# Normalized rows plus projection bias kept in DRAM, and a last stage in five parts

## The chip, the cores and the metric

The kernel runs on one core of a Trainium2 chip. The time is device time in microseconds (us) of one execution, as the median of several runs. The engines are named as in the profile: PE (TensorE, matmuls; PEld is its weight load), DVE (VectorE), ACT (ScalarE), POOL (GpSimd), and SP (SyncE, which here only issues transfers). Each engine takes its instructions in program order, and waits for another engine or for a transfer by semaphores.

## What is computed

Two transformer layers over four sequences of 512 rows of 512 numbers (2048 rows in all, float32). Each layer normalizes its input and adds an attention and a mixture of experts, both taken from the same normalized rows. Only layer 1 is touched:

```python
xn = _layernorm(x)
x = x + _L1_attn_ref(xn, ...) + _L1_ffn_ref(xn, ...)

def _L1_ffn_ref(x, router_w, router_b, expert_w, expert_b, proj_w, proj_b, norm_w):
    logits = einsum('bsd,de->bse', x, router_w) + router_b
    topk_vals, topk_idx = top_k(logits, 2)
    topk_w = softmax(topk_vals)
    ...
    expert_out = silu(einsum('td,edf->etf', xf, expert_w) + expert_b[:, None, :])
    combined = ...            # the two chosen experts' rows, weighted with topk_w
    out = einsum('bsd,df->bsf', combined, proj_w) + proj_b
    y = x + out               # x is the normalized row here
    rms = sqrt(mean(y * y) + 1e-6)
    return norm_w * (y / rms)
```

What the change moves is `x + proj_b`, the sum of the normalized row and the projection's bias.

## The kernel before

The rows lie in 16 tiles of 128 rows x 512 (`NT` = 16, number `n`). `acc` (in SBUF) holds the residual stream, `xnT` the transposed normalized rows of a layer.

**Layer 0** runs in 32 steps (8 groups of head pairs x 4 sequences). `schedule` hangs further jobs into places `(step, place)` of this loop: router, experts, and from step 29 on the start of layer 1. `next_layer(n)` (L938) makes tile n's normalized rows of layer 1: `layernorm` (L215) writes `xn` on DVE (L236), stores it to `xnd` in DRAM (L237), and `turn` transposes it on PE. Then POOL adds the attention's output bias to `acc` (L944) and SP stores that to `accd`. The expert stage of layer 1 gathers its inputs from `xnd`. Tiles 0 to 11 have this in steps 29 to 31; tiles 12 to 15 in the boundary between the layers (from L1428), where it alternates with `values(0, t)`, the first value products. In the same steps POOL computes the scalars of layer 0's query norms (L565, L566), which ACT (L675) and then DVE wait for. `begin_combine` (L908) loads the constants that these jobs use, and its pool `comb` holds one buffer of each kind.

**Layer 1** is a loop over 16 groups `g` of heads and 4 blocks `kc` of keys, 64 places `at[0]` to `at[63]`. A place has score products (L1224), two exponentials on ACT (`pT`, L1226), the context products (L1238) and, on DVE, sums of the exponentials (`pS`, L1244), with projections of the next group (`queries7`, L1200) and of the next sequence's values (`values7`, L1160 to L1174) in between. The values of the last sequence are made in places 46 and 47. Jobs hang into these places too: 36 expert tiles, which store their rows to `yd` in DRAM (L527), and then the mixing stage.

**Mixing stage**, for each tile n: `mix` gathers the two experts' rows of each token from `yd` with two indirect transfers on POOL (L534), loads the normalized rows from `xnd` (`xa`), weights the first row with its gate on DVE (L1340) and adds the second, weighted, on DVE (L1341), while POOL adds the projection bias to `xa` (L1342). `turn_mix` transposes the mixture on PE (L1349) and ACT evicts it (L1354). `project_mix` multiplies with the projection on PE (L1360), DVE adds the result to `xa` (L1361), ACT squares and sums, POOL makes the norm scalars (L1365, L1366). `finish_mix` scales on DVE (L1371) and adds to the output (L1296). The four parts of tile n hang at places `here` to `here + 3`, with `here = 48 + n * 13 // 16`. Row buffers and `xa` are double.

**Order.** The source fixes which job hangs where. The order of instructions on each engine is set by a scheduler, which may move an instruction before earlier ones of the source, unless it is pinned with `tc.keep_in_program_order`. In `mix` the first weightings of tiles 0 and 1 are pinned (L1339). PSUM banks are handed round: a matmul into a bank waits for the read of what lay in it before (`bank1("mm", ...)` for the products of values, queries, attention output and mixing alike).

A second path for very large scores stands further down in the file and is not touched.

Of the kernel before, what the change touches and what calls it, by code (L numbers as in the profile page):

```python
# [49 lines left out]
def two_layers(ctx: ExitStack, tc: tile.TileContext, a: dict, out: bass.AP, large: bass.AP):  # L50
# [80 lines left out]
    xnd = dram.tile([T, HID], F32, tag="xnd", name="xnd")  # L131
    yds = [dram.tile([NS * P, HID], F32, tag=f"yd{i}", name=f"yd{i}") for i in range(2)]

    accd = dram.tile([T, HID], F32, tag="accd", name="accd")

    def load_x(n):
# [75 lines left out]
        tc.keep_in_program_order(V.memset(turned, 1.0))  # L212
        V.tensor_scalar(turned[R:P, :], wcol[R:P, 0:1], wcol[R:P, 1:2], D * math.sqrt(D), ALU.mult, ALU.mult)

    def layernorm(n, pool, bank, scaled=False):  # L215

        pin = tc.keep_in_program_order if n < TC else (lambda x: x)
        st = small.tile([P, 6], F32, tag="st", name=f"st_{n}")  # L220
        pin(V.bn_stats(st, acc[:, n, :]))
        mv = small.tile([P, 2], F32, tag="mv", name=f"mv_{n}")
        V.bn_aggr(mv, st)
        V.tensor_scalar(mv[:, 1:2], mv[:, 1:2], 1e-5, None, ALU.add)
        G.tensor_tensor(mv[:, 1:2], mv[:, 1:2], nhalf[:, 0:1], ALU.pow)
        if scaled:
            G.tensor_scalar(mv[:, 0:1], mv[:, 0:1], mv[:, 1:2], -1.0, ALU.mult, ALU.mult)
        made = {}

        def rows():  # L230
            tag = "ctx" if n in (2, 3) else "xn"
            xn = made["xn"] = (wk0 if n in (2, 3) else pool).tile([P, HID], F32, tag=tag, name=f"xn_{n}")
            if scaled:
                A.activation(xn, acc[:, n, :], AF.Identity, scale=mv[:, 1:2], bias=mv[:, 0:1])
            else:
                pin(V.tensor_scalar(xn, acc[:, n, :], mv[:, 0:1], mv[:, 1:2], ALU.subtract, ALU.mult))  # L236
            (nc.scalar if TC <= n < 2 * TC else nc.sync).dma_start(out=xnd[ts(n, P), :], in_=xn)  # L237

        def turn():
            xn, tr = made["xn"], bank("tr", f"trx_{n}")  # L240
            for k in range(KC):
                pin(PE.transpose(tr[:, ts(k, P)], xn[:, ts(k, P)], ident))
            A.copy(xnT[:, :, ts(n, P)], tr.rearrange("p (k t) -> p k t", k=KC))
        return rows, turn


    def logits(b, w, m, pool, name, get, bank):
# [660 lines left out]
    def begin_combine():  # L908

        scratch.close()  # L910
        first = ctx.enter_context(tc.tile_pool(name="first1", bufs=1, side="right"))
        load_square(first, "wvT")
        rout["rw"] = load_few(first, "rw", E, a["rw"])
        rout["rb"] = load(first, "rb", [P, E], a["rb"].partition_broadcast(P))
        rout["wo_b"] = load(first, "wo_b", [P, HID], a["wo_b"].partition_broadcast(P))
        rout["pool"] = scratch.enter_context(tc.tile_pool(name="comb", bufs=1, side="right"))
        rout["ex"].pool = rout["pool"]
# [18 lines left out]
        jobs0.append((at[n + 1], lambda n=n: rout.pop(n)()))  # L936

    def next_layer(n, pool, bank):  # L938
        make_rows, turn_ = layernorm(n, pool, bank)

        def rows():
            make_rows()

            G.tensor_tensor(acc[:, n, :], acc[:, n, :], rout["wo_b"], ALU.add)  # L944
            nc.sync.dma_start(out=accd[ts(n, P), :], in_=acc[:, n, :])
        return rows, turn_

    norms = {}
# [376 lines left out]
    def begin_mixing():  # L1325
        scratch.close()
        rout["mix"] = scratch.enter_context(tc.tile_pool(name="mix", bufs=2, side="right"))
        rout["ex1"].pool = rout["mix"]
        load_square(rout["mix"], "pw")
        for nm in ("pb", "nw1"):  # L1330
            rows[nm] = load(rout["mix"], nm, [P, HID], a[nm].partition_broadcast(P))

    def mix(n):

        g0, g1 = rout["ex1"].gather(n)
        x = rout["mix"].tile([P, HID], F32, tag="xr", name=f"xa_{n}")
        nc.sync.dma_start(out=x, in_=xnd[ts(n, P), :])

        pin = tc.keep_in_program_order if n < 2 else (lambda x: x)  # L1339
        pin(V.tensor_scalar(g0, g0, r1.gate[:, 0, n : n + 1], None, ALU.mult))  # L1340
        V.scalar_tensor_tensor(g0, g1, r1.gate[:, 1, n : n + 1], g0, ALU.mult, ALU.add)  # L1341
        G.tensor_tensor(x, x, rows["pb"], ALU.add)  # L1342
        held[n] = g0, x

    def turn_mix(n):
        g0, x = held[n]
        tr = bank1("mm", f"trc_{n}")
        for f in range(KC):
            PE.transpose(tr[:, ts(f, P)], g0[:, ts(f, P)], ident)  # L1349
# [6 lines left out]
    def project_mix(n):  # L1356
# [2 lines left out]
        for f in range(KC):  # L1359
            PE.matmul(op, lhsT=cT_[:, f, :], rhs=wa["pw"][:, f, :], start=(f == 0), stop=(f == KC - 1))  # L1360
        V.tensor_tensor(y, y, op, ALU.add)  # L1361
        sq = rout["mix"].tile([P, HID], F32, tag="th", name=f"ysq_{n}")
        ss = small.tile([P, 1], F32, tag="yss", name=f"yss_{n}")
        A.activation(sq, y, AF.Square, accum_out=ss)
        G.tensor_scalar(ss, ss, 1.0 / HID, 1e-6, ALU.mult, ALU.add)  # L1365
# [29 lines left out]
    for i, here in enumerate(here_):  # L1395
# [4 lines left out]
                ex.fetch_weights(j + 3)  # L1400
            ex.fetch_bias(i + 2)
        jobs1.append((at[here], after))
    first += 6 + NS * 11 // 12
    jobs1.append((at[first], begin_mixing))
    for n in range(NT):
        here = first + n * 13 // 16
        for d, f in ((0, mix), (1, turn_mix), (2, project_mix), (3, finish_mix)):
            jobs1.append((at[here + d], lambda n=n, f=f: f(n)))

    left_ = sums_qk()  # L1410
    for place, f in (((1, 1), left_[0]), ((1, 2), left_[1]), ((1, 3), left_[2]), ((2, 0), sums_v), ((2, 1), left_[3])):
# [4 lines left out]
        jobs1.append((place, lambda t=t: values(1, t)))  # L1416
    run1 = schedule(jobs1)

    values(0, 0)
    norm = [next_layer(3 * TC + t, rp, bank1) for t in range(2)]  # L1420
    norm[0][0]()
    values(0, 1)
    turn_ = second_logits(B - 2, rp, bank1)
    norm[0][1]()
    norm[1][0]()
    norm.append(next_layer(3 * TC + 2, rp, bank1))
    values(0, 2)
    turn_()  # L1428
    norm[1][1]()
    norm[2][0]()  # L1430
    norm.append(next_layer(3 * TC + 3, rp, bank1))
# [752 lines left out]
```

## Time and profile before

| what | value |
|---|---|
| median of 3 runs | 2073.92 us (2073.34 to 2074.24) |
| the profiled execution | 2074.66 us, its span 2072.6 us, PE clock 0.995 |
| busy PE / weight load / DVE / ACT / POOL | 2017.7 / 1205.3 / 1452.0 / 867.9 / 754.3 us |
| layer 0 / boundary / layer 1 | to about 1451 / 1451 to 1480 / from 1480 us |
| last expert rows stored, first gather of mixing issued | 1881.73 us |
| HBM read and written | 222.05 MB and 42.73 MB, 128 GB/s over the span |

Most groups of instructions of the mixing stage, and what the change adds to elsewhere, have simple durations when they stand alone:

| line | engine | what | us of one |
|---|---|---|---|
| L1340 | DVE | weight the first row | 0.48 |
| L1341 | DVE | add the second, weighted | 0.75 |
| L1342, L944 | POOL | add a bias, 128x512 | 1.26, 1.27 |
| L1354 | ACT | evict the transposed mixture, 128x512 | 0.60 |
| L1226 | ACT | exponential, 128x1024 | 1.01 |
| L1244 | DVE | sum of exponentials, 128x1024 | 1.22 |
| L534 | POOL | issue a gather of 128 rows | 1.16 mean |
| `accd`, `xnd` | SP | store of 256 KB, issue to landing | 2.0 median |

How to read the profile: a line of a timeline gives the start in us from the span's beginning, the duration, the engine, the source line, the operation, output <- inputs by the program's names, shapes, and, in brackets, how long the engine stood idle just before and what it waited for. A line of a window gives its bounds, its length, then the busy time (and number of instructions) of PE, PEld, DVE, ACT and POOL, the granted PE clock, the share of the DMA engines' time that was busy, and GB/s. A duration that is longer than the same instruction's elsewhere says that something held it while it ran; idle time in brackets says that something held it before it started. Idle time of an engine other than PE matters only where PE later waits for it.

### The profile page before, as it was taken

How to read it: one execution, taken by the hardware profiler on the slowest of the kernel's cores; microseconds unless marked ns; L12 is line 12 of the kernel's file. 1: busy time of each engine (PE TensorE's matmuls, PEld its weight loads, DVE VectorE, ACT ScalarE, POOL GpSimd, SP SyncE). 2: the span in 40 equal slices, each digit the busy share in tenths (PEclk: the TensorE clock that was granted, in tenths of full speed). 3: DMA queues.
4: the chain of work that ended last, by engine and by line, in shares of the span. 5: the costliest groups of instructions: out<-in, count | busy, mean ns of one | idle time of the engine just before them, and what ended most of it. 6: DMA issues, size and time to landing. Idle time of an engine off the chain costs nothing.

```text
span 2072.6 us, 27984 instructions
## 1 busy us (share of the span) xinstructions
PE 2017.7 (97%) x9130; PEld 1205.3 (58%) x9130; DVE 1452.0 (70%) x3543; ACT 867.9 (42%) x2600; POOL 754.3 (36%) x761
## 2 busy tenths in 40 slices
PE   6999999999999999999999999999999999999997
PEld 4666666666666666666666666666334445445442
DVE  7888967666766666676667778787596555557775
ACT  4554444444444443444444455454243432333332
POOL 4422244443423333344333444353114332332550
PEclk9999999999999999999999999999999999999999
DMA  7102133333333343234443222121317765773551
GB/s 250 68 31 62 42 118 120 143 108 103 130 130 104 109 155 103 92 135 166 183 170 116 70 76 85 42 72 62 119 51 244 263 243 196 257 243 123 158 163 52
DMA packets 98906, 267.23 MB, mean 129 GB/s; under 512 B 14400, under 2 KB 27840, under 8 KB 87488
## 3 DMA queue, kind: packets, MB, share of 16 engines
q0 software_dynamic: 27072, 148.91, 21.4%
q1 hardware_dynamic: 70528, 114.34, 16.4%
q10 hardware_dynamic: 1152, 2.10, 0.3%
q8 instruction: 75, 1.23, 0.2%
q14 instruction: 79, 0.65, 0.1%
HBM read 222.05 MB, written 42.73 MB: 128 GB/s over the span
## 4 chain that ended last, share of the span: by engine, by line
PE 81%; DVE 8%; ACT 3%; POOL 2%; DMA 2%; issue 1%; SPq 0%; ACTq 0%; POOLq 0%; DVEq 0%
PE p L661 23%; PE hp_r L518 12%; PE op L828 10%; PE st L753 4%; PE st L1224 3%; PE qp L1200 3%; PE sp L744 3%; PE cx L1238 2%; PE ca L797 2%; PE o L1307 2%; PE trm_r L506 2%; PE vp L1160 1%; PE trq L681 1%; PE trk L687 1%; PE cc L800 1%
## 5 line engine op out<-in xcount | busy, mean ns | idle before, releaser
L828 PE MATMUL op<-Wo,cT 128*128 128x512 f32 x512 | 230.6, 598 | 5.3 <-DVE lv L725 2.9
L518 PE MATMUL hp_r<-we_r,xT_r 128*128 128x512 f32 (+1 forms) x592 | 224.8, 596 | 0.0
L470 POOL DMA_INDIRECT xr_r<-xnd,rows_r x72 | 89.4, 1242 | 331.6 <-PE trm_r L506 298.2
L761 POOL TENSOR_TENSOR lT<-lT,lmask 128x512 f32<-128x512 f32 (+1 forms) x128 | 157.6, 1244 | 140.8 <-ACT lT L757 140.6
L661 PE MATMUL p<-wT,x 128*128 128x384 f32 x512 | 179.6, 493 | 0.5 <-DVE wT L119 0.5
L661 PE MATMUL p<-wB,x 128*128 128x384 f32 x512 | 175.9, 488 | 4.0 <-DVE u L717 4.0
L661 PE MATMUL p<-wA,xnT 128*128 128x384 f32 x512 | 174.0, 492 | 0.2 <-DVE u L696 0.2
L828 PEld LDWEIGHTS op<-Wo,cT 128*128 128x128 f32 x512 | 92.0, 190 | 115.0 <-issue 77.2
L564 ACT ACTIVATE sq<-qb 128x128 f32<-128x128 f32 x384 | 118.9, 310 | 93.0 <-DVE qb L710 44.9
L1226 ACT ACTIVATE pT<-st 128x1024 f32<-128x1024 f32 x128 | 123.7, 1014 | 62.7 <-PE st L1224 57.0
L518 PEld LDWEIGHTS hp_r<-we_r,xT_r 128*128 128x128 f32 (+1 forms) x592 | 83.8, 170 | 97.3 <-issue 91.8
L831 DVE TENSOR_TENSOR acc<-acc,op 128x512 f32<-128x512 f32 x128 | 87.4, 685 | 69.4 <-PE op L828 69.0
L661 PEld LDWEIGHTS p<-wB,x 128*128 128x128 f32 x512 | 93.9, 190 | 68.5 <-issue 10.2
L661 PEld LDWEIGHTS p<-wT,x 128*128 128x128 f32 x512 | 94.5, 193 | 63.5 <-issue 6.7
L661 PEld LDWEIGHTS p<-wA,xnT 128*128 128x128 f32 x512 | 95.6, 193 | 61.0 <-issue 2.9
L675 ACT ACTIVATE qb<-qb,ss 128x128 f32<-128x128 f32 x256 | 81.9, 390 | 110.7 <-POOL ss L566 108.6
L508 ACT COPY xT_r<-trm_r 128x512 f32<-128x512 f32 x72 | 41.8, 581 | 198.0 <-PE hp_r L518 188.3
L757 ACT ACTIVATE lT<-st,ss 128x256 f32<-128x256 f32 (+1 forms) x128 | 47.2, 449 | 175.4 <-PE st L753 175.3
L753 PE MATMUL st<-qkT 128*128 128x256 f32 (+1 forms) x512 | 110.4, 357 | 0.0
L534 POOL DMA_INDIRECT row_r<-yd,slot_r x64 | 74.2, 1160 | 94.0 <-DVE row_r L1341 35.8
L753 PEld LDWEIGHTS st<-qkT 128*128 128x128 f32 x512 | 93.1, 193 | 11.4 <-issue 1.4
L566 POOL TENSOR_TENSOR ss<-ss,nhalf 128x6 f32<-128x6 f32 x64 | 95.7, 1496 | 5.3
(360 smaller groups left out, 4334.2 us busy)
## 6 DMA issues: line engine op xcount, KB each, us to landing
x<-xsd SPq DMA_DIRECT2D x112, 256.0 KB, 3.1
yd<-yr_r SPq DMA_DIRECT2D x72, 256.0 KB, 3.4
wA<-in_wA SPq DMA_DIRECT2D x16, 384.0 KB, 3.6
wB<-in_wB SPq DMA_DIRECT2D x16, 384.0 KB, 7.6
xnd<-xn SPq DMA_DIRECT2D x24, 256.0 KB, 2.0
accd<-acc SPq DMA_DIRECT2D x18, 256.0 KB, 2.0
acc<-in_x SPq DMA_DIRECT2D x16, 256.0 KB, 4.9
Wo<-in_Wo SPq DMA_DIRECT2D x8, 512.0 KB, 3.6
```

What stands on the lines that cost most here:

```text
L470: G.indirect_dma_start(out=out, out_offset=None, in_=src, in_offset=at_rows(idx))
L518: PE.matmul(hp[ts(h, m), :], lhsT=xT[:, k, ts(h, m)], rhs=w[:, ts(k, HID)], start=(k == 0), stop=(k == KC - 1))
L534: G.indirect_dma_start(out=x, out_offset=None, in_=self.yd, in_offset=at_rows(self.r.slot[:, k, n : n + 1]))
L564: A.activation(sq, x[:, h, :], AF.Square, accum_out=ss[:, h : h + 1])
L566: G.tensor_tensor(ss, ss, nhalf[:, 0:n], ALU.pow)
L661: PE.matmul(p, lhsT=x[:, k, ts(c, P)], rhs=w[:, k, :], start=(k == 0), stop=(k == 1))
L675: A.activation(x[:, j, :], x[:, j, :], AF.Copy, scale=sq[t][:, j : j + 1])
L753: PE.matmul(st[:, ds((t % 2) * 256, n)], lhsT=qkT[:, HG + h, ts(t, P)], rhs=qkT[:, h, ds(t * P, n)], start=True, stop=True)
L761: G.tensor_tensor(dst, dst, lmask.rearrange("p a w j -> p (a w j)")[:, 0:n], ALU.mult)
L828: PE.matmul(op, lhsT=cT[:, h, ts(t, P)], rhs=wo[:, h, :], start=(h == 0), stop=(h == HG - 1))
L831: V.tensor_tensor(acc[:, n, :], acc[:, n, :], op, ALU.add)
L1226: A.activation(pt[:, ts(pair, 2), :], st, AF.Exp, scale=SCALE1)
```

## The change

Where layer 1's normalized rows are made (`next_layer`), POOL now also forms `xp = xn + pb`, tile by tile in one buffer, and SP stores it to a new DRAM tensor `xpd`. For this `pb` is loaded with the constants of `begin_combine`. In the mixing stage `xa` is loaded from `xpd`, and the POOL addition of the bias is gone.

The stage has five parts instead of four: `gather_mix` (the two gathers), `mix` (weighting: the first row now on ACT, a copy with a scale, the second on DVE as before), `turn_mix` (now also loads `xa`, in four buffers), `project_mix`, `finish_mix`. The stage begins one place earlier, at `at[47]`. For tiles 0 to 2 the gathers hang at 47, 47 and 48 and the weighting at 49; from tile 3 on the weighting, transposes, projection and finish are at the places where they were. The first row has three buffers instead of two, the square's scratch one instead of two, and the pin of the first weightings is gone. The norm's weights go into the buffer of the attention's output bias, which is free by then.

In the boundary between the layers, the normalizations of tiles 12 and 13 are set up before `values(0, 0)`, and the router's logits of sequence 2 are made before `values(0, 1)` and finished right behind it.

```diff
@@ setup
+    xpd = dram.tile([T, HID], F32, tag="xpd", name="xpd")
@@ layernorm
-    def layernorm(n, pool, bank, scaled=False):
+    def layernorm(n, pool, bank, scaled=False, made=False):
...
-        made = {}
+        of, made = made, {}
...
-        return rows, turn
+        return (rows, turn, made) if of else (rows, turn)
@@ begin_combine
         rout["rb"] = load(first, "rb", [P, E], a["rb"].partition_broadcast(P))
+        rout["pb"] = load(first, "pb", [P, HID], a["pb"].partition_broadcast(P))
         rout["wo_b"] = load(first, "wo_b", [P, HID], a["wo_b"].partition_broadcast(P))
@@ next_layer
-        make_rows, turn_ = layernorm(n, pool, bank)
+        make_rows, turn_, rows_ = layernorm(n, pool, bank, made=True)
...
             G.tensor_tensor(acc[:, n, :], acc[:, n, :], rout["wo_b"], ALU.add)
             nc.sync.dma_start(out=accd[ts(n, P), :], in_=acc[:, n, :])
+
+            xp = pool.tile([P, HID], F32, tag="xp", name=f"xp_{n}")
+            G.tensor_tensor(xp, rows_["xn"], rout["pb"], ALU.add)
+            nc.sync.dma_start(out=xpd[ts(n, P), :], in_=xp)
@@ -1325,25 +1332,29 @@
     def begin_mixing():
         scratch.close()
         rout["mix"] = scratch.enter_context(tc.tile_pool(name="mix", bufs=2, side="right"))
-        rout["ex1"].pool = rout["mix"]
         load_square(rout["mix"], "pw")
-        for nm in ("pb", "nw1"):
-            rows[nm] = load(rout["mix"], nm, [P, HID], a[nm].partition_broadcast(P))
+
+        rows["nw1"] = rout["wo_b"]
+        nc.sync.dma_start(out=rows["nw1"], in_=a["nw1"].partition_broadcast(P))
+
+    def gather_mix(n):
+
+        held[n] = []
+        for k in range(2):
+            x = rout["mix"].tile([P, HID], F32, tag=f"row{k}", name=f"row{k}_r1_{n}", bufs=3 - k)
+            G.indirect_dma_start(out=x, out_offset=None, in_=yds[1], in_offset=at_rows(r1.slot[:, k, n : n + 1]))
+            held[n].append(x)
 
     def mix(n):
 
-        g0, g1 = rout["ex1"].gather(n)
-        x = rout["mix"].tile([P, HID], F32, tag="xr", name=f"xa_{n}")
-        nc.sync.dma_start(out=x, in_=xnd[ts(n, P), :])
-
-        pin = tc.keep_in_program_order if n < 2 else (lambda x: x)
-        pin(V.tensor_scalar(g0, g0, r1.gate[:, 0, n : n + 1], None, ALU.mult))
+        g0, g1 = held[n]
+        A.activation(g0, g0, AF.Copy, scale=r1.gate[:, 0, n : n + 1])
         V.scalar_tensor_tensor(g0, g1, r1.gate[:, 1, n : n + 1], g0, ALU.mult, ALU.add)
-        G.tensor_tensor(x, x, rows["pb"], ALU.add)
-        held[n] = g0, x
 
     def turn_mix(n):
-        g0, x = held[n]
+        g0, _ = held[n]
+        x = rout["mix"].tile([P, HID], F32, tag="xr", name=f"xa_{n}", bufs=4)
+        nc.sync.dma_start(out=x, in_=xpd[ts(n, P), :])
         tr = bank1("mm", f"trc_{n}")
         for f in range(KC):
             PE.transpose(tr[:, ts(f, P)], g0[:, ts(f, P)], ident)
@@ -1359,7 +1370,7 @@
         for f in range(KC):
             PE.matmul(op, lhsT=cT_[:, f, :], rhs=wa["pw"][:, f, :], start=(f == 0), stop=(f == KC - 1))
         V.tensor_tensor(y, y, op, ALU.add)
-        sq = rout["mix"].tile([P, HID], F32, tag="th", name=f"ysq_{n}")
+        sq = rout["mix"].tile([P, HID], F32, tag="th", name=f"ysq_{n}", bufs=1)
         ss = small.tile([P, 1], F32, tag="yss", name=f"yss_{n}")
         A.activation(sq, y, AF.Square, accum_out=ss)
         G.tensor_scalar(ss, ss, 1.0 / HID, 1e-6, ALU.mult, ALU.add)
@@ -1400,12 +1411,14 @@
                 ex.fetch_weights(j + 3)
             ex.fetch_bias(i + 2)
         jobs1.append((at[here], after))
-    first += 6 + NS * 11 // 12
+    first += 5 + NS * 11 // 12
     jobs1.append((at[first], begin_mixing))
     for n in range(NT):
         here = first + n * 13 // 16
-        for d, f in ((0, mix), (1, turn_mix), (2, project_mix), (3, finish_mix)):
-            jobs1.append((at[here + d], lambda n=n, f=f: f(n)))
+        for d, f in ((0, gather_mix), (1, mix), (2, turn_mix), (3, project_mix), (4, finish_mix)):
+
+            place = max(here + d, first + 1 + d + (n > 2)) if d else here
+            jobs1.append((at[place], lambda n=n, f=f: f(n)))
 
     left_ = sums_qk()
     for place, f in (((1, 1), left_[0]), ((1, 2), left_[1]), ((1, 3), left_[2]), ((2, 0), sums_v), ((2, 1), left_[3])):
@@ -1416,16 +1429,16 @@
         jobs1.append((place, lambda t=t: values(1, t)))
     run1 = schedule(jobs1)
 
+    norm = [next_layer(3 * TC + t, rp, bank1) for t in range(2)]
     values(0, 0)
-    norm = [next_layer(3 * TC + t, rp, bank1) for t in range(2)]
     norm[0][0]()
+    turn_ = second_logits(B - 2, rp, bank1)
     values(0, 1)
-    turn_ = second_logits(B - 2, rp, bank1)
+    turn_()
     norm[0][1]()
     norm[1][0]()
     norm.append(next_layer(3 * TC + 2, rp, bank1))
     values(0, 2)
-    turn_()
     norm[1][1]()
     norm[2][0]()
     norm.append(next_layer(3 * TC + 3, rp, bank1))
```

## The prediction

> **What bounds the kernel now.** I read the page's busy totals and the chain that ended last, then windows by stage, then each engine's timeline where TensorE (PE) idles. Totals and chain:
>
> ```profile
> PE 2017.7 (97%) x9130; PEld 1205.3 (58%) x9130; DVE 1452.0 (70%) x3543; ACT 867.9 (42%) x2600; POOL 754.3 (36%) x761
> ...
> PE 81%; DVE 8%; ACT 3%; POOL 2%; DMA 2%; issue 1%; SPq 0%; ACTq 0%; POOLq 0%; DVEq 0%
> ```
>
> PE is the bound: 2017.7 of 2072.6 us. The edit leaves its matmuls alone, so it acts only through PE's idle time and granted clock. Windows (us, then busy time of PE, weight loads, DVE, ACT, POOL, then PE clock, DMA share, GB/s), for the end of layer 0, the start of mixing, and mixing:
>
> ```profile
> 1400.00:1450.00 50.00, 46.49 (x248) 31.04 (x248) 38.70 (x115) 22.67 (x71) 18.94 (x18) 1.00 0.17 64
> 1878.00:1905.00 27.00, 27.00 (x144) 16.62 (x136) 16.22 (x25) 8.15 (x10) 6.99 (x7) 1.00 0.42 147
> 1960.00:2020.00 60.00, 54.60 (x220) 25.15 (x213) 41.65 (x59) 22.10 (x40) 34.52 (x37) 0.97 0.53 158
> 2020.00:2051.00 31.00, 27.43 (x113) 9.33 (x112) 22.75 (x31) 10.86 (x20) 4.99 (x8) 1.00 0.14 49
> ```
>
> PE has no hole while mixing starts (27.00 of 27.00) and loses 9.0 us between 1960 and 2051. That 9.0 is what can be won; the hole-free 27 us are what can be spoilt. PE's waits from 1905 to 2051, totalled (us, times, longest), then two pieces of its timeline (start, us, line, in brackets the idle time and what ended it):
>
> ```profile
> PE po L1360 <- DVE acc L1296: 2.1, 1, 2.1
> PE qp L1200 <- DVE xnT L1296: 2.0, 1, 2.0
> PE st L1224 <- ACT pT L1226: 1.7, 1, 1.7
> PE po L1360 <- DVE xa L1361: 1.6, 3, 0.6
> ```
>
> ```profile
> 1889.40 1.89 PE L1160 MATMUL vp<-acc 128*128 128x256 f32 x8
> 1891.13 1.89 PE L1160 MATMUL vp<-acc,xnT 128*128 128x256 f32 x8
> 1892.85 3.60 PE L1307 MATMUL o<-woT,cT 128*128 128x512 f32 x8
> ```
>
> ```profile
> 1973.13 3.12 PE L1200 MATMUL qp<-xnT,wqT 128*128 128x256 f32 x8 [2.01 <-DVE xnT L1296]
> 1976.06 1.62 PE L1200 MATMUL qp<-acc 128*128 128x256 f32 x4
> ```
>
> The last pair took 3.12 and 1.62 us; the same matmuls at 1898.45 and 1900.28, behind no stall, took 1.99 and 1.03. So PE ran slow after the stall: 1.7 us more. Three waits (2016.60, 1973.13, 2035.70) hold most of the idle time.
>
> **Removed: work in the mixing stage.** Sixteen DVE weightings (L1340, 0.48 us, 7.7 us in all) go to ACT, and sixteen POOL additions (L1342) go. The additions cost more than their own time where they meet DVE. DVE, then POOL:
>
> ```profile
> 1968.40 2.29 DVE L1244 TENSOR_TENSOR pS<-pS,pT 128x1024 f32<-128x1024 f32 x1
> ```
>
> ```profile
> 1968.18 1.42 POOL L1342 TENSOR_TENSOR xa<-xa,pb 128x512 f32<-128x512 f32 x1 [1.61 <-DVE acc L1296]
> ```
>
> The pS addition beside L1342 took 2.29 us, alone (1971.27) 1.21: 1.08 lost. Stall by stall: before 1973.13 the DVE chain held one L1340 (0.48) and that 1.08, so 1.56 of 2.01 goes, and with so short a stall the 1.7 of slow clock: 3.25. Before 2016.60 L1341 took 1.76 instead of 0.75 beside L1342, and one L1340 stood in the queue: 1.5. The 1.67 at 2035.70 (0.9 of slow matmuls behind it) goes back to POOL's norm scalars, queued behind an L1342 for which POOL had idled 6.04 until its rows landed at 2025.74; DVE and ACT stand between, so I take half, 1.3. Three stalls on the residual addition L1361 (0.25, 0.47, 0.60) lose about 1.0. Sum 7.05; less 0.5 for ACT's added op, **-6.5 us**. Ends: all eight stalls of the stage with their slow clock, 8.9 + 4.7 = -13.6; only the two collisions, 1.08 + 1.01 = -2.1. The added ACT op has no row; its nearest are the 128x512 evictions combT (0.60) and ysq (0.63): 0.6. In steady state it stands between two exponentials (1.01 each) and waits for a gather whose buffer a transpose frees: 0.3 to issue + 3.7 to land + 0.6 + 1.0 = 5.6 us, against 9.56 from one transpose to the next (1918.92 to 1928.48). PE's own work covers it by 4 us, and I exclude a loss there.
>
> **Added: rows plus bias in layer 0 and at the boundary.** Per tile one POOL addition (nearest row L944, same size: 1.27 us) and one 256 KB store on SP (like accd: 2.0 us to land), with one buffer. Twelve fall in layer 0's last steps, where POOL is 38% busy and hides most. Tile 5's does not hide: the new program order puts it ahead of L565/L566, on which a chain to PE hangs. POOL, then DVE, then PE:
>
> ```profile
> 1406.98 1.51 POOL L944 TENSOR_TENSOR acc<-acc,wo_b 128x512 f32<-128x512 f32 x1 [7.69 <-DVE xn L236]
> ```
>
> ```profile
> 1407.28 1.43 DVE L574 TENSOR_TENSOR r<-qb,t 128x192 f32<-128x192 f32 x1
> 1408.63 0.35 DVE L575 TENSOR_TENSOR r<-qb,t 128x192 f32<-128x192 f32 x1
> ```
>
> ```profile
> 1413.94 1.56 PE L661 MATMUL p<-wB,x 128*128 128x384 f32 x4 [0.48 <-DVE u L717]
> ```
>
> L565 (1408.58, right behind L944) moves by 1.27; behind it ACT's scaling, DVE's L813 and L717 move too, and PE, already idle 0.48 there, gets +1.27. DVE is 77% busy (38.70 of 50), and L574 beside L944 took 1.43, its equal L575 0.35: again 1.08. I put one more such collision on PE's path: **+2.35**. Ends: 0 (no collision, and the chain's slack larger than the trace lets see) and 1.27 + 3 x 1.08 = +4.5, a collision at each of the three larger PE stalls of that stretch.
>
> [...]
>
> At the boundary tile 11's new store (waiting for POOL's addition, about 1455.2) goes into SP's queue ahead of three weight loads. wkT was issued at 1454.35 and wv_b at 1455.82, both now some 1.4 us later; v's addition (DVE L1148), which waited for wv_b until 1466.07, moves with it, and tile 12's rows wait for the pool that the store holds (1458.44 to about 1460.5). PE's stalls there (0.80, 0.68, 0.83, 0.68, 0.80) are on those engines, and tile 13's DVE rows now also wait for the single buffer. The new order of the four normalizations gives part back: **+1.6**, ends 0 and +4, both transfers' delay one after the other.
>
> **Moved: the first weightings.** Before, those of tiles 0 and 1 were pinned and ran at 1903.01, long after their rows had landed. The pin is gone. The changed program has DVE's first three combinations (successors of L1341) between the additions of values: L1165, combine 0, L1166, combine 1, L1167, combine 2, L1168, two pS, L1170. ACT's three weightings stand ahead of the next pair of exponentials. The rows cannot come earlier, since POOL waits for the last expert store:
>
> ```profile
> 1881.73 1.15 POOL L534 DMA_INDIRECT row_r<-yd,slot_r  x1 [21.74 <-DMA yd<-yr_r]
> 1883.18 0.95 POOL L534 DMA_INDIRECT row_r<-yd,slot_r  x1 [0.30 <-issue]
> ```
>
> The transfers issued from 1880 to 1892 show what that costs (last number: median us from issue to landing; two loads of xa beside them took 9.1):
>
> ```profile
> row_r<-yd,slot_r POOLq DMA_INDIRECT x4, 7.4
> ```
>
> Combine 0 needs the second gather: 1883.18 + 7.4 = 1890.6, + 0.75 = 1891.3; L1166 (0.69) then ends at 1892.0, and the vp product that reuses its bank starts at 1892.1 instead of 1889.40. Combine 1 has the fourth: 1885.69 + 7.4 = 1893.1, with L1167 to 1894.5. Combine 2's second row reuses combine 0's buffer: issued 1891.4, landing after 3.7 (the later median) at 1895.1; combine 2 to 1895.8, L1168 to 1896.4, two pS (2.36) to 1898.7, L1170 to 1899.3. PE's L1307 waits for L1170's bank: 1899.35 instead of 1892.85, 6.5 late. A stall of 2 us cost 1.7 of slow clock at 1973 and 0.07 at 2016.60; I take 1.0: **+7.5**. Ends: 3.3 to land, the shortest later gather, puts L1170 at 1895.7, +2.9 with no slow clock; 9.1 for the first and 4.8 (slowest later) for the last make 9.3 + 1.7 = +11.0.
>
> [...] The row at 1973.13 shows slowing after 2.0 us already. [...]
>
> **Sum.** +2.35 + 1.6 + 7.5 - 6.5 = +4.95 on the profiled span: 2072.6 + 4.95 = 2077.55; around the span lie 2.06 us (2074.66 in all), so 2079.6. The profiled run is 0.74 above the median of 2073.92, so **2078.9**.
>
> **Rivals.** What can be told from no change is 0.2%, 4.15 us: 2069.8 to 2078.1.
> A, faster: the first gathers land as fast as the later ones (3.3 to 3.7), since the bias no longer loads beside them. The start then costs 2.9, and DVE, ahead of its queue, leaves no stall in the stage: 2073.9 + 2.35 + 1.6 + 2.9 - 13.6 = 2067.2. It decides below about 4.4 us to landing. For it: DVE and POOL end the stage's stalls. Against: the new order queues four row loads beside the first gathers, the same 2 MB. 0.22.
> B, within 0.2%: the same early landing with my gain of 6.5: 2074.4. 0.20.
> C, larger loss: the ACT weighting, behind slow gathers, also holds the exponentials later on, so the stage gives 2.1 only and the five parts do not run ahead as their number says (a row buffer still comes free at a transpose): 2073.9 + 2.35 + 1.6 + 7.5 - 2.1 = 2083.3. For it: landing at 7.4 makes the 5.6 us chain 9.3 of 9.56. Against: later gathers land in 3.7. 0.13.
> The forecast has 0.45.
>
> **Numbers.** All low ends give 2065.8, all high ends 2091.3; 8 in 10 lie between 2067 and 2087. Slower: the forecast, most of it, and C, less small parts on the line: 0.54; within 0.2%: 0.22; faster: 0.24. The forecast's own range is 2075 to 2084.
>
> **What would show it.** Right: PE idle before vp at about 1890 and before L1307, named after the combinations or their gathers; DVE idle there on a DMA; no 2.01 at qp. Wrong: no idle of PE from 1878 to 1905 (then A or B), or idle at exponentials behind the ACT weighting in every group (C). In layer 0, no extra 1.3 at L661's stall would drop the first term.

## The result, and the profile after

The changed kernel takes 2079.06 us (median of 14 runs, 2076.41 to 2083.78) against 2074.07 (14 runs, 2070.62 to 2079.67). The ratio is 1.0021, 95% interval 1.0014 to 1.0028: slower by 2.9 to 5.8 us. Its profiled execution has a span of 2075.7 us, 3.1 more than before. (Two places in the description above: the eviction of the transposed mixture is on L1353, and the boundary begins with L1419.) Lines of the changed kernel stand 2 to 13 higher than the same lines before: L1340 is now ACT's L1351, L1341 is L1352, L1166 is L1173, L1170 is L1177, L1307 is L1314, L1360 is L1371.

Busy totals of the changed kernel, then four windows. They begin 2 to 5 us later than the windows of the kernel before. The work itself comes 1 to 14 us later at their bounds (worked out as in the table further down), so they tell where the holes are and not what each of them costs:

```profile
PE 2018.1 (97%) x9130; PEld 1205.8 (58%) x9130; DVE 1441.8 (69%) x3527; ACT 878.1 (42%) x2616; POOL 748.5 (36%) x761
```

```profile
1405.00:1452.00 47.00, 40.81 (x224) 28.06 (x223) 34.16 (x101) 21.07 (x65) 26.22 (x24) 0.96 0.27 99
1880.00:1907.00 27.00, 22.36 (x104) 13.80 (x101) 17.72 (x24) 6.44 (x8) 7.76 (x8) 0.94 0.47 166
1963.00:2023.00 60.00, 58.83 (x245) 26.64 (x248) 43.51 (x61) 28.18 (x49) 25.66 (x30) 1.00 0.50 153
2023.00:2054.00 31.00, 30.41 (x136) 10.65 (x129) 23.52 (x32) 13.81 (x25) 2.96 (x8) 1.00 0.19 62
```

The holes have moved. Between 1963 and 2054 PE now idles 1.8 us instead of 9.0, while mixing's start, which had none, has 4.6 us of idle time at a clock of 0.94. Layer 0's end has become worse too: PE idles 6.2 us of 47 at a clock of 0.96. In the kernel before it was 3.5 us of 45 at 1.00:

```profile
1405.00:1450.00 45.00, 41.49 (x229) 27.94 (x228) 35.68 (x106) 21.00 (x65) 18.94 (x18) 1.00 0.19 71
```

More exact than windows is a ledger. PE runs the same matmuls in all kernels here, so each one's start can be set against its start in the kernel before; how much later it comes, at the two ends of a stretch, tells what the stretch lost (+) or gave back (-). Worked out so from the traces, in us, with the stretches named by the times of the kernel before:

| kernel | layer 0, 1340-1425 | 1425-1444 | boundary, to 1482 | layer 1, to 1885 | mixing's start, to 1898 | to 1930 | mixing, to 2055 |
|---|---|---|---|---|---|---|---|
| before, a second trace | +0.26 | +0.01 | +0.01 | -0.43 | 0.00 | 0.00 | +1.16 |
| changed | +3.54 | +1.57 | +1.10 | -0.18 | +6.85 | +0.96 | -10.76 |
| pin3 | +3.53 | +3.21 | +1.38 | +0.16 | 0.00 | +5.89 | -11.11 |
| natural | +3.55 | +1.40 | +1.33 | +0.81 | 0.00 | 0.00 | -10.59 |
| xp_only | +3.54 | +3.22 | +0.54 | -0.14 | 0.00 | 0.00 | -6.68 |
| five_only | +0.23 | +2.79 | -1.19 | +0.85 | +13.20 | +0.83 | -5.65 |
| natural_xnd | +0.25 | -0.01 | -1.19 | -0.42 | 0.00 | 0.00 | -5.47 |
| pin3_xp_late | +0.23 | +3.13 | -1.20 | +30.92 | 0.00 | +4.79 | -10.57 |
| natural_late | +0.24 | -0.02 | -1.20 | -0.30 | 0.00 | 0.00 | -9.30 |
| late_dve | +0.23 | +3.16 | -1.20 | +0.48 | 0.00 | 0.00 | -9.28 |
| store_only | -0.08 | +1.37 | +4.59 | +1.02 | +6.84 | +0.93 | -10.56 |
| xa_pinned | +3.29 | +1.60 | +1.05 | -0.05 | +4.85 | +1.03 | -9.93 |
| old_boundary | +3.53 | +3.23 | +0.29 | -0.40 | +6.96 | +0.94 | -10.63 |

Where the work is the same the figures of the first and third to sixth columns repeat to some 0.5 us (layer 1's, to 1); mixing's differ by 1.2 between the two traces of the kernel before; the second column is spoken of at the end. How late PE is at 1340 already (-1.8 to +1.5 in these traces) is not in the table, so a row need not add up to the difference in span. Mixing's start in the changed kernel, POOL, DVE and PE:

```profile
1888.42 0.94 POOL L1345 DMA_INDIRECT row_r<-yd,slot_r  x1 [22.47 <-PE vp L1167]
1889.67 0.95 POOL L1345 DMA_INDIRECT row_r<-yd,slot_r  x1 [0.30 <-issue]
```

```profile
1896.96 0.75 DVE L1352 SCALAR_TENSOR_TENSOR row_r<-row_r,gate_r,row_r 128x512 f32<-128x512 f32 x1 [7.54 <-DMA row_r<-yd,slot_r]
1897.62 0.68 DVE L1173 TENSOR_TENSOR xnT<-vp,xnT 128x512 f32<-128x512 f32 x1
...
1901.30 0.75 DVE L1352 SCALAR_TENSOR_TENSOR row_r<-row_r,gate_r,row_r 128x512 f32<-128x512 f32 x1 [1.46 <-DMA row_r<-yd,slot_r]
...
1904.84 0.68 DVE L1177 TENSOR_TENSOR v<-xnT,vp 128x512 f32<-128x512 f32 x1
```

```profile
1893.54 1.99 PE L1167 MATMUL vp<-wvT,acc 128*128 128x256 f32 x8
1898.37 3.30 PE L1167 MATMUL vp<-acc 128*128 128x256 f32 x8 [2.83 <-DVE xnT L1173]
1901.46 2.31 PE L1167 MATMUL vp<-acc,xnT 128*128 128x256 f32 x8
1905.58 3.70 PE L1314 MATMUL o<-woT,cT 128*128 128x512 f32 x8 [1.80 <-DVE v L1177]
```

DVE stands 7.54 us in front of the first combination, which starts at 1896.96, when the rows of the second gather, issued at 1889.67, have landed. Behind it stands L1173, which reads the bank that PE's next value product needs: PE idles 2.83, then 1.80, and its products take 3.30 and 2.31 us instead of 1.89.

### The profile page after: what moved, and what is told of

The parts are those of the page before. It is cut to its first block, busy times and chain, and to the rows that moved or that the text cites. A ratio compares the mean times of both kernels' runs of the same rounds, so it can differ in the third digit from the quotient of the medians.

```text
span 2075.7 us, 27993 instructions
## 1 busy us (share of the span) xinstructions
PE 2018.1 (97%) x9130; PEld 1205.8 (58%) x9130; DVE 1441.8 (69%) x3527; ACT 878.1 (42%) x2616; POOL 748.5 (36%) x761
## 4 chain that ended last, share of the span: by engine, by line
PE 81%; DVE 7%; ACT 3%; POOL 2%; issue 2%; DMA 2%; ACTq 0%; DVEq 0%; POOLq 0%; SPq 0%
PE p L663 23%; PE hp_r L520 12%; PE op L830 10%; PE st L755 4%; PE st L1231 3%; PE qp L1207 3%; PE sp L746 3%; PE cx L1245 2%; PE ca L799 2%; PE trm_r L508 2%; PE o L1314 2%; PE po L1371 1%; PE trq L683 1%; DMA row_r<-yd,slot_r 1%; PE trk L689 1%
## 5 line engine op out<-in xcount | busy, mean ns | idle before, releaser
L830 PE MATMUL op<-Wo,cT 128*128 128x512 f32 x512 | 231.4, 600 | 5.3 <-DVE lv L727 3.2
L830 PEld LDWEIGHTS op<-Wo,cT 128*128 128x128 f32 x512 | 92.2, 190 | 115.1 <-issue 77.2
L567 POOL TENSOR_SCALAR ss<-ss 128x6 f32<-128x6 f32 x64 | 32.0, 500 | 165.2 <-ACT sq L566 165.0
```

The source lines that it names most:

```text
L830: PE.matmul(op, lhsT=cT[:, h, ts(t, P)], rhs=wo[:, h, :], start=(h == 0), stop=(h == HG - 1))
```

## The experiments

Ratios and totals are given against executions of the kernel before in the same session. before_again, store_only, xa_pinned and old_boundary were executed once each, so only their traces are read.

**Four variants, first round.** pin3 holds the early weightings at their places in the source:

```diff
-        A.activation(g0, g0, AF.Copy, scale=r1.gate[:, 0, n : n + 1])
-        V.scalar_tensor_tensor(g0, g1, r1.gate[:, 1, n : n + 1], g0, ALU.mult, ALU.add)
+        pin = tc.keep_in_program_order if n < 3 else (lambda x: x)
+        pin(A.activation(g0, g0, AF.Copy, scale=r1.gate[:, 0, n : n + 1]))
+        pin(V.scalar_tensor_tensor(g0, g1, r1.gate[:, 1, n : n + 1], g0, ALU.mult, ALU.add))
```

> The changed kernel, with the weightings of tiles 0 to 2 held at their place in the source. Theory (the early combinations block VectorE, and through it PE): the idle times of PE of 2.83 and 1.80 us at the value products and at the attention output of mixing's start, and the slow matmuls between them, go. Over the stretch from the score products at 1885 to the attention output at 1895 (clock of the kernel before) PE loses 0 to 0.5 us against the kernel before instead of 6.85; total 5 to 8 us below the changed kernel, so about 2072. Rival (the rows land late in any case, so the wait only moves to the first transposes of the mixture): PE idles some 3 to 6 us at the first transposes instead, total within 2 us of the changed kernel.

Measured: 1.0012 (1.0003 to 1.0022), 2077.21 us. The 6.85 at mixing's start is gone, and 5.89 comes back 22 to 25 us later: the rival was right about the total, which lies 1.9 us below the changed kernel's. PE of pin3:

```profile
1920.49 1.12 PE L1231 MATMUL st<-qk 32*128 32x512 f32 x2 [1.45 <-ACT pT L1233]
1923.33 1.12 PE L1361 MATMUL trc<-ident,row_r 128*128 128x128 f32 x4 [1.72 <-DVE row_r L1353]
```

The diff puts tiles 0, 1 and 2 at the same places, and the second row has two buffers: tile 2's gather waits for tile 0's combination, which now comes late (1916.76). So its row is the one that PE's transpose waits for. The early weightings had hidden that second bill.

xp_only is the kernel before with the sum alone (`xp` and its store in `next_layer`, `xa` loaded from `xpd`, L1342 gone); five_only is the changed kernel without it:

```diff
-            xp = pool.tile([P, HID], F32, tag="xp", name=f"xp_{n}")
-            G.tensor_tensor(xp, rows_["xn"], rout["pb"], ALU.add)
-            nc.sync.dma_start(out=xpd[ts(n, P), :], in_=xp)
...
-        nc.sync.dma_start(out=x, in_=xpd[ts(n, P), :])
+        nc.sync.dma_start(out=x, in_=xnd[ts(n, P), :])
+        G.tensor_tensor(x, x, rout["pb"], ALU.add)
```

> The kernel before with only the sum kept in DRAM: POOL adds the bias where the rows are made, SP stores the sum, mixing loads it and has no addition; four parts, VectorE weightings, pins and boundary order of the kernel before. Theory: layer 0 late by about 5.05 us as in the changed kernel, boundary by 1 to 2.5 (old order), mixing's start by 0 to 0.5, mixing gives back 4 to 8 us; total 2071 to 2077. Rival A (the loss in layer 0 is an accident of the changed kernel's whole order): layer 0 late by under 2.5. Rival B (the removed additions are nothing to the gain in mixing): mixing gives back under 2 us, total 2079 or more.

> The changed kernel without the sum kept in DRAM: normalized rows are loaded in mixing and POOL adds the bias there, as in the kernel before; five parts, the ScalarE weighting, and the order at the boundary stay. Theory (the additions and their stores cost layer 0 its 5.05 us, through POOL and VectorE): layer 0 is within 0.1 us of the kernel before; at mixing's start PE still loses 6 to 7.5 us; mixing gives back only 1 to 5 us, since POOL's additions meet VectorE's as before. Total 2074 to 2080. Rival A (layer 0's loss is from something else in the diff): layer 0 stays late by 3 us or more. Rival B (the gain in mixing is that of the ScalarE weighting alone): mixing gives back 9 us or more.

Measured: xp_only 0.9997 (0.9988 to 1.0007), five_only 1.0045 (1.0028 to 1.0062). The sum costs layer 0 3.3 to 3.55 us up to 1425 wherever it is made there, and five_only has 0.23: that loss belongs to it. In mixing the sum alone gives 6.68, the five parts without it 5.65, both together 10.8. Neither rival of xp_only held; its boundary (0.54) lies below the range. five_only misses its ranges. Its layer 0 is late by 3.02 in all, which by the number alone meets its rival A; but 2.79 of it fall between 1425 and 1444, although nothing is added there, and the end of this text tells of that stretch. Mixing (5.65) lies above its range. And at mixing's start it loses 13.2, because POOL's additions now run beside the early combinations. DVE, POOL and PE of five_only there:

```profile
1895.46 2.09 DVE L1348 SCALAR_TENSOR_TENSOR row_r<-row_r,gate_r,row_r 128x512 f32<-128x512 f32 x1 [0.38 <-DMA row_r<-yd,slot_r]
...
1898.13 3.73 DVE L1348 SCALAR_TENSOR_TENSOR row_r<-row_r,gate_r,row_r 128x512 f32<-128x512 f32 x1
```

```profile
1898.81 2.49 POOL L1354 TENSOR_TENSOR xa<-xa,pb 128x512 f32<-128x512 f32 x2
```

```profile
1906.45 6.05 PE L1310 MATMUL o<-woT,cT 128*128 128x512 f32 x8 [6.25 <-DVE v L1173]
```

The second and third combinations take 2.09 and 3.73 us instead of 0.75; PE idles 6.25 us before the attention output instead of 1.80, and the products behind take 6.05 instead of 3.70.

pin3_xp_late moves the sum into layer 1, through the buffer of a bias that is free by then:

```diff
+    def add_pb(n):
+        x = rout["wo_b"]
+        nc.sync.dma_start(out=x, in_=xnd[ts(n, P), :])
+        G.tensor_tensor(x, x, rout["pb"], ALU.add)
+        nc.sync.dma_start(out=xpd[ts(n, P), :], in_=x)
...
+    for n in range(NT):
+        jobs1.append((at[first + 2 + 2 * n], lambda n=n: add_pb(n)))
```

> As pin3, but the sum of rows and bias is made in layer 1, one tile every two places of the loop from place 11 on (load the normalized rows, POOL adds, store), where PE idles 0.9 us of 398 and POOL is busy 30%; nothing is added to layer 0 or to the boundary. Theory: layer 0 within 0.1 us of the kernel before, boundary within 1, layer 1 up to mixing late by 0 to 2, mixing's start 0 to 0.5, mixing gives back 9 to 11 us; total 2062 to 2067, faster than both. Rival (POOL's queue is in order, and an addition that waits for its load holds up the expert gathers behind it): layer 1 late by 3 us or more, total 2068 to 2076.

Measured: 1.0133 (1.0116 to 1.0150). The rival, and worse than it: layer 1 lost 30.9. POOL's waits in it, from 1510 to 1600 (total, times, longest):

```profile
POOL wo_b L1331 <- DMA wo_b<-xnd: 53.8, 11, 5.8
```

The scheduler had put all sixteen additions, from 1479.5 to 1575.7, ahead of the expert gathers but one, each with a load and a store to wait for in the one buffer.

**Second round: places, and the sum where there is room.** natural gives every tile its places as before, with the gathers one earlier, and keeps pin3's pins:

```diff
-            place = max(here + d, first + 1 + d + (n > 2)) if d else here
+            place = here + d
```

> The changed kernel with the parts of all tiles at here + 0 to here + 4 (so the weightings of tiles 0 to 2 hang at places 48, 48 and 49 as in the kernel before, and only the gathers come earlier) and those weightings held there. Theory (the loss at mixing's start is that of weightings before their rows have landed, and in pin3 of three tiles at one place with two buffers for the second row): PE loses 0 to 1.5 us from 1885 to 1930 against the kernel before, instead of 8.4 in the changed kernel and 5.9 in pin3; mixing gives back 9 to 11.5; layer 0 and the boundary are late as in the changed kernel (5 to 8). Total 2069 to 2073. Rival (the five parts need the head start, and without it mixing has stalls as in the kernel before): mixing gives back under 6, total over 2075.

Measured: 0.9979 (0.9970 to 0.9989), 2071.21 us. Nothing is lost from 1885 to 1930, and mixing gives back 10.59. So 7.8 us of the change (6.85 + 0.96) lay in three tiles' places and a missing pin. Window of natural over mixing's start:

```profile
1885.00:1912.00 27.00, 27.00 (x141) 16.72 (x137) 15.63 (x22) 9.48 (x12) 5.77 (x6) 1.00 0.46 157
```

natural_xnd takes the sum out of natural, as five_only did; natural_late makes it in layer 1 with the load a place ahead and all three steps held (`load_row` at `first + 2 + 2 * n`, `add_pb` at `first + 3 + 2 * n`, each under `keep_in_program_order`).

> As natural, but without the sum in DRAM: normalized rows are loaded in mixing and POOL adds the bias there. Theory: layer 0 up to 1425 late by 0.2 instead of 3.5, the boundary early by 1.2; mixing's start 0 to 3; mixing gives back 5 to 8 (with the additions beside VectorE again). Total 2067 to 2073. Rival (without the sum in DRAM POOL's additions, waiting for their loads, hold the gathers behind them, as the 13.2 us at mixing's start of five_only let fear): mixing's start loses over 5, total over 2074.

> As natural, but the sum of rows and bias is made in layer 1, one tile every two places from place 11 on; the load hangs one place (about 9.6 us) ahead of the addition, and loads, additions and stores are held at their places, since without this the scheduler had put ten additions in a row ahead of the expert gathers (31 us lost). Theory: no such loss (layer 1 late by 0 to 2), layer 0 up to 1425 late by 0.2, the boundary early by 1.2, 2 to 3 for the fetch beside the store, mixing as in natural. Total 2062 to 2068, faster than both. Rival (POOL's additions collide with VectorE all through layer 1): layer 1 late by 4 us or more, total over 2069.

Measured: natural_xnd 0.9984 (0.9972 to 0.9995). natural_late 0.9943 (0.9926 to 0.9959), 2063.69 us: 8.5 to 15.4 us faster than the kernel before. Sixteen additions in layer 1 cost nothing that the ledger shows (-0.30); POOL is busy for 30% of layer 1 in the kernel before. natural_xnd loses nothing at mixing's start, so its rival fell; five_only's additions needed the early, crowded weightings beside them to do harm. natural and natural_xnd are equally fast within their intervals: made in layer 0, the sum wins 5.1 us in mixing and loses 7.2 before 1482.

before_again is the kernel before once more:

> The kernel before once more, for a second trace of it. In the changed kernel and in all four variants so far VectorE waits at its sums (L1116 of the kernel before) for tile 6's store to accd some 2 us longer than in the first trace of the kernel before, also where nothing is added to layer 0; each time a 16 KB instruction fetch lies beside that store's packets. Theory (the fetch falls where the code puts it, so it belongs to the program and not to chance): the fetch starts more than 1 us before the store's packets again, as in the first trace (1431.42 against 1433.28), and PE's stalls from 1425 to 1444 are within 0.3 us of it. Rival (chance): the fetch lies beside the store in this trace too, or the loss there differs by over 1 us.

Measured: its stretch from 1425 to 1444 is the same (+0.01), but the fetch came at 1434.25, right after the store's packets and not 1.9 us ahead of them. So where the fetch falls moves by some 3 us between executions, and whether it meets the store is at least partly chance; the theory that the program fixes it fell.

**Third round: single terms.** late_dve is natural_late with `V.tensor_scalar(g0, g0, r1.gate[:, 0, n : n + 1], None, ALU.mult)` in place of the ScalarE copy.

> As natural_late, with the first row's weighting on VectorE (0.48 us each) instead of ScalarE: tells what the ScalarE weighting is worth in the mixing stage. Theory (the stage's stalls came of POOL's additions beside VectorE and of loads they waited for, and VectorE has room once they are gone): mixing gives back 8 to 10.5 us against 10.2 in natural_late, total 2062 to 2067. Rival (VectorE's queue is what holds PE there, and the 16 weightings are the larger part of the gain): mixing gives back under 7, total 2067 or more.

Measured: mixing -9.28 against -9.30 in the table (the expectation says 10.2), 0.9964 (0.9950 to 0.9978). ScalarE's weighting is worth nothing in sum once the additions are gone. (This trace has the fetch's 3.16.)

store_only keeps the store and drops the addition:

```diff
-            xp = pool.tile([P, HID], F32, tag="xp", name=f"xp_{n}")
-            G.tensor_tensor(xp, rows_["xn"], rout["pb"], ALU.add)
-            nc.sync.dma_start(out=xpd[ts(n, P), :], in_=xp)
+            nc.sync.dma_start(out=xpd[ts(n, P), :], in_=rows_["xn"])
```

> The changed kernel without POOL's additions in layer 0 and at the boundary: SP stores the normalized rows themselves to the new tensor, right where the sum was stored. It leaves out the projection bias. Theory (POOL's additions, their place ahead of the norm scalars and their collisions with VectorE make layer 0's loss): PE is late by 0.5 us or less at 1425 instead of 3.5, and by 0 to 3 at 1444 (the fetch); the boundary, where the stores queue ahead of the weight loads, loses 0.5 to 1.5 as before. Rival (the stores, 4 MB more on SP's queue and the DMA engines, make it): late by 2 us or more at 1425.

Measured: -0.08 up to 1425, where the changed kernel has +3.54: POOL's additions make that loss, not the stores. The boundary lost 4.59 and so missed its range. PE idles 1.2 to 1.3 us there before the transposes of three tiles (1471.16, 1476.49, 1481.88) whose rows DVE makes only behind its additions of values; why they come so late in this variant was not shown, so it does not tell what the stores alone cost the boundary.

xa_pinned holds the loads of `xa` for tiles 0 to 3 (`pin(nc.sync.dma_start(...))` for n < 4):

> The changed kernel with the loads of xa for tiles 0 to 3 held at their place in the source, behind the attention output's store, so that 1 MB less is under way beside the first gathers. Theory (the gathers land late because of the loads beside them): the first two gathers land 4 to 6 us after their issue instead of some 7.2, and PE's loss from the score products at 1885 to the attention output at 1893 falls from 6.85 to between 2.5 and 5.5. Rival (the landing is the gathers' own time, or that of the 1 MB of projection weights ahead): landing within 0.7 us of 7.2, loss within 1 us of 6.85.

Measured: the first combination's rows, from a gather issued at 1889.63, have landed by 1894.71 (5.1 us at most; 7.3 in the changed kernel), and the loss is 4.85 instead of 6.85. The loads beside the gathers make part of their time. PE of xa_pinned:

```profile
1896.12 1.99 PE L1167 MATMUL vp<-acc 128*128 128x256 f32 x8 [0.84 <-DVE xnT L1173]
...
1903.31 3.70 PE L1314 MATMUL o<-woT,cT 128*128 128x512 f32 x8 [3.47 <-DVE v L1177]
```

old_boundary puts the old order of the boundary back:

> The changed kernel with the boundary's old order of normalizations, value products and router logits. Theory (without the added stores the new order saves 1.2 us, as the variants without the sum in layer 0 show; with them tile 11's and 12's stores take that back): the stretch from 1456 to 1482 loses 0.3 to 1.0 us, against 1.1 in the changed kernel, so the new order does not pay there. Rival (the new order pays in the changed kernel too): the stretch loses 2.0 us or more.

Measured: +0.29 against +1.10. Without the sum the new order gains 1.2 (five_only, natural_xnd, natural_late); with it the new order loses 0.8 more than the old (0.5 to 1.1 if the other kernels with the sum are taken in).

## Why the prediction was right, and where it was not

The total, 2078.9 against 2079.06, and the side are right, and so is the largest loss and its mechanism. That the total fits to 0.2 us is luck, for two terms were well off, in opposite directions, one of them beyond its end. On the trace the terms are 3.54 + 1.57 + 1.10 - 0.18 + 6.85 + 0.96 - 10.76 = +3.08, against +4.95 worked out. The medians of 14 runs are 4.99 apart, because the profiled run of the changed kernel lies 1.5 us below its median and that of the kernel before 0.6 above; chance in the second column (0 to 3.2) is of that size. In the working itself all low ends add up to 2063.2, not 2065.8, and rival B to 2074.25, not 2074.4; the forecast does not rest on either.

**First weightings: right, but for the slow clock.** +7.5 was worked out, +6.85 measured: the two large stalls stand before the two PE instructions named, for the reason named, and landing took 7.3 against 7.4. L1314 starts at 1905.58, where L1307 stood at 1892.85; PE was 5.97 late already, so the stalls put it off by 6.76, against 6.5 worked out. The 1.0 added for slow matmuls was not lost. The slow products (1.41 and 0.42 longer, at a granted clock of 0.58 and 0.85) ran in time in which PE would have waited: VectorE, busy without a gap from the third combination at 1901.30 to the end of L1177, let L1314 start. L1314's own products take 3.70 instead of 3.60, and 6.76 + 0.10 is the 6.85. xa_pinned moved the loss the way the landing moved, with no slow products before L1314. Rivals A and B needed rows that land in 3.3 to 3.7 us, and fell with that. What the forecast had not priced is the 0.96 behind it, a projection waiting 1.28 for DVE behind tile 5's combination, which had waited 1.51 for its rows; with pin3 the same crowding of tiles 0 to 2 costs 5.89. "PE's own work covers it by 4 us" was worked out for the steady state and does not hold where three tiles stand at one place.

**Rows plus bias in layer 0: mis-sized.** The term was +2.35 with an upper end of 4.5; measured 5.11 over both stretches of layer 0, of which 3.3 belongs to the additions for certain (3.54 against 0.23 without them) and the 1.57 is shared with a fetch of instructions, told of at the end. The place was right: tile 5's addition pushes the norm scalars. POOL, DVE and PE of the changed kernel, then PE's first transposes in the kernel before:

```profile
1407.79 1.52 POOL L947 TENSOR_TENSOR acc<-acc,wo_b 128x512 f32<-128x512 f32 x1 [7.88 <-DVE xn L238]
1409.27 1.39 POOL L951 TENSOR_TENSOR xp<-xn,pb 128x512 f32<-128x512 f32 x1
1410.74 0.20 POOL L567 TENSOR_SCALAR ss<-ss 128x6 f32<-128x6 f32 x1
```

```profile
1408.09 1.43 DVE L576 TENSOR_TENSOR r<-qb,t 128x192 f32<-128x192 f32 x1
1409.45 1.42 DVE L577 TENSOR_TENSOR r<-qb,t 128x192 f32<-128x192 f32 x1
```

```profile
1416.23 1.60 PE L663 MATMUL p<-wB,x 128*128 128x384 f32 x4 [1.96 <-DVE u L719]
1417.63 1.06 PE L683 MATMUL trq<-ident,qb 128*128 128x128 f32 x4
1418.48 1.06 PE L689 MATMUL trk<-ident,qb 128*128 128x128 f32 x4
```

```profile
1415.33 0.60 PE L681 MATMUL trq<-ident,qb 128*128 128x128 f32 x4
```

L577, 0.35 us before, now takes 1.42 beside `xp`, as L576 does beside L947, and L567 starts at 1410.74, 1.35 later on the matmuls' clock. PE's idle time goes from 0.48 to 1.96: the 1.48 is what the step "+1.27" foresaw. Missed is what follows: behind 1.96 us of idle time the transposes take 1.06 us instead of 0.60, at a granted clock of 0.50, and the stretch is 1.2 longer for it. The forecast put in such a price at mixing's start, where it was not lost, and left it out here, where it was. A further 0.63 is lost at 1377, where the output projection (L830, L828 before) now waits for DVE; 1.48 + 1.2 + 0.63 are the 3.3.

**Boundary: nearly right.** +1.6 against +1.10. The queue of stores ahead of the weight loads showed (wkT is issued at 1460.61 instead of 1454.35, of which 5.05 is lateness from layer 0); the part that the new order "gives back" it did not give back, by old_boundary.

**Mixing: mis-sized, the larger error.** -6.5 was taken; -10.76 measured, within the end of -13.6. The step that failed is the weighing stall by stall. Half was taken of the 1.67 at 2035.70 and nothing of the two stalls behind it, and of four stalls on L1361 one (0.47 at 2008.30) was left out. PE of the kernel before:

```profile
2035.70 2.04 PE L1224 MATMUL st<-qk 32*128 32x512 f32 x8 [1.67 <-ACT pT L1226]
...
2042.90 1.97 PE L1238 MATMUL cx<-pT,v 128*32 128x512 f32 x8 [0.53 <-ACT pT L1226]
...
2045.55 2.19 PE L1252 MATMUL sm<-pS,ones 128*32 128x512 f32 x8 [0.68 <-DVE pS L1244]
```

The ledger gives 2.63 between 2030 and 2037 and 1.69 between 2037 and 2046, so those went whole: 4.3 us where 1.3 was taken. The last two are not the additions' doing: xp_only has no additions in the stage and keeps both (0.53 and 0.68; nothing won from 2037 to 2046), while five_only and natural_xnd, which have the additions and five parts, win 1.65 and 1.76 there. The forecast priced the weightings and additions that leave the stage and put the five parts themselves (earlier gathers, more buffers) at nothing. What remains in the stage is small, PE's waits from 1909 to 2054 in the changed kernel:

```profile
PE po L1371 <- DVE xnT L1303: 1.3, 1, 1.3
PE po L1371 <- ACT rsum L1264: 0.8, 2, 0.5
PE trc L1360 <- DVE qk L1212: 0.7, 1, 0.7
PE sm L1259 <- DVE pS L1251: 0.5, 1, 0.5
```

The gain was also put down to the wrong edits in part. The 0.48 us weightings, counted in two of the stalls, are worth nothing in sum (late_dve). The additions' removal is worth 6.68 alone, the five parts without it 5.5, together 9.3 to 11: they clear in part the same stalls and do not add. Which of the five parts' edits (earlier gathers, more buffers) gives the 5.5 was not separated. Rival C, exponentials held up by the ScalarE weighting all through the stage, did not happen: none of the waits above is on exponentials.

How a POOL addition slows one on VectorE beside it was not shown, only the time (L577: 1.42 us beside a POOL addition of 1.39, 0.35 before). PE's slow matmuls can be read in the granted clock: behind 1.96 us of idle time it was 0.50 (1.06 us instead of 0.60), behind 2.83 it was 0.58 (3.30 instead of 1.89), behind the 2.01 at 1973.13 in the kernel before 0.61 (3.12 instead of 1.99). Behind the 2.13 at 2016.60 it was 1.00, and 3.47 us in xa_pinned were followed by 3.70 instead of 3.60. The length of the one stall does not tell here whether matmuls run slow behind it, and where they did, in three places, they took 0.6 to 0.9 of the stall's length longer (1.2 behind 1.96, 1.7 behind 2.01, 1.8 behind 2.83).

## What to carry to other kernels

When work leaves a crowded stage, look for where it lands: the same additions cost 3.3 us at layer 0's end, ahead of a chain that PE waits for, and nothing in the middle of layer 1 (-0.30 in natural_late). An instruction that waited for a transfer was a wall here for everything behind it on its engine (7.54 us of VectorE in the changed kernel, 53.8 us of POOL in pin3_xp_late), so a scheduler that moves it ahead must be held until the transfer can have landed; and holding it is of use only if buffers and places behind it let it start there (pin3 lost nothing at mixing's start and 5.89 us behind it, natural 0.00 at both). In the kernel before a stall of 2.01 us on TensorE cost 1.7 us more in slow matmuls (at 1973.13, granted clock 0.61), and one of 2.13 us 0.07 (at 2016.60, granted clock 1.00); at mixing's start of the changed kernel 1.83 us of slow matmuls cost nothing, since TensorE would have waited anyway.

## What the runs showed of the hardware

One loss belongs to no edit. VectorE's L1116 (L1119, L1121 or L1123 in the other kernels) waits for a store of 256 KB to `accd`. Transfers issued from 1432 to 1438 in natural_late and in five_only, with the rate in 40 slices:

```profile
GB/s 0 0 0 0 0 0 0 0 123 396 410 369 369 82 0 0 0 0 0 0 0 0 0 0 0 0 0 0 0 0 0 0 0 0 0 0 0 0 0 0
...
q1 hardware_dynamic: 144, 0.26, 11.6%
...
accd<-acc SPq DMA_DIRECT2D x1, 256.0 KB, 2.0
```

```profile
GB/s 0 0 0 0 0 0 0 0 0 0 0 232 369 437 396 287 28 0 0 0 0 0 0 14 14 0 14 14 27 27 0 0 0 0 0 0 0 0 0 0
...
q1 hardware_dynamic: 144, 0.26, 11.9%
q8 instruction: 1, 0.02, 1.6%
```

And DVE of five_only:

```profile
1437.09 0.69 DVE L1119 TENSOR_TENSOR acc<-wvT,acc 128x512 f32<-128x512 f32 x1 [2.16 <-DMA accd<-acc]
```

In five_only one 16 KB fetch of instructions, 1.54 us long, runs beside the store; most of the store has gone through, and a thin rest (14 to 27 GB/s) follows 1 to 2 us later. VectorE gets past its wait 4.2 us after the store's issue at 1432.88, where the store in natural_late landed after 2.0, and PE loses 2.79. In all fourteen traces it is so: with a fetch beside the store VectorE waits 1.6 to 2.3 us for it (nine traces), without one 0.34 or less (five). That the fetch delays the store is read from this, and no run moved the fetch alone. Of seven traces without the sum in layer 0 three show this (five_only, late_dve, pin3_xp_late, 2.8 to 3.2 us), the other four lose nothing there. With the sum in layer 0 natural, whose fetch ended 0.6 us before the store's first packet, loses 1.40, so that much seems to be the sum's own; the five others (changed, pin3, xp_only, xa_pinned, old_boundary) have a fetch beside the store and lose 1.6 to 3.2. store_only, with no addition but a second store, has a fetch beside the store and loses 1.37, less than the three. One trace without the fetch is thin ground for that division. Such a fetch comes about every 27 us in layer 0 (52 of them up to 1451 in the kernel before), and its time against the program differs by some 3 us between executions of one kernel (1431.42 and 1434.25 in the kernel before). It may be one source of the spread of single runs; that was not shown.
